# Two buffers for the column marks, one PSUM tile for both halves of the count, and the count one slot later

## The chip, the cores and the metric

One core of a Trainium2 chip runs the whole network as one launch. The metric is the time on the device in microseconds (us), for the slowest core, which here is the only one.

## What is computed

Four graph layers run over the same 4096 nodes of 256 features and the same 4096 x 4096 matrix `adj`; each ends in a layer norm. The change lies in layer 1, in the first of its two attention steps:

```python
def _top_p_attention(X, W1, W2, W3):
    q = X @ W1.T @ W2.T
    k = X @ W3.T
    probs = jax.nn.softmax(q @ k.T / TAU, axis=-1)
    idx = jnp.argsort(-probs, axis=-1)
    sp = jnp.take_along_axis(probs, idx, axis=-1)
    cs = jnp.cumsum(sp, axis=-1)
    keep_sorted = cs - sp < TOP_P            # 0.9
    ...
    A = probs * mask
    return A / jnp.maximum(A.sum(-1, keepdims=True), 1e-12)
...
for n in range(2):
    A = _top_p_attention(Xa, W1, W2, W3)
    Xf = R @ Xf                              # R: adj-like matrix, rows sum to 1
    Xa = A @ Xa
    Z = Z + Xf @ U1[n].T + Xa @ U2[n].T
```

Each row keeps its largest probabilities until they sum to 0.9. In the first step few columns are kept, so the kernel lists the columns that any row of a block needs and gathers only those.

## The kernel before

**Blocks and steps.** The first attention step is a stage of its own. It handles 32 blocks (`I`) of 128 rows. `narrow(I)` is a Python generator that writes one block's instructions; each `yield` ends a step. A loop by hand advances every live block by one step in each slot, the oldest block first, and starts a new block every 8 slots (`SLOTS`). A block lives about 42 slots, so five or six blocks are interleaved, and eight slots make a round. Beside them `r_stream()` advances 1.15 steps a slot (`PACE`): it gathers rows of `qtab` by lists (`xg`, on POOL, line 379) and multiplies them into `acc` (line 1156) three of its own steps later (`LATE`). For the later blocks it also gathers `pc`, blocks of `adj`. The order on PE, ACT, DVE and POOL is the order written (`manual_schedule`); only the DMAs on SP are placed by the scheduler.

**A block's steps around the change**, numbered from its start:

- 0 to 8: logits `lg` of 2 x 512 columns on PE (line 1014), their exp `e` on ACT (1029), and the eight largest of each 256 columns on DVE (`cand`, 1020), four times.
- 9 and 10: the 40 largest are sorted on DVE (`top`, `rest`), and a threshold `mid` between the last kept and the first dropped is found. `ex` is the running sum of the 40; POOL copies its last value to `f_x` (1043).
- 11 to 15: the change is here. ACT writes `marks` = sign(mid - e) in bf16 for 2048 of the 4096 columns (1056). PE counts them: for each 128 columns, `marks` is the weight and a column of ones the moving operand, so that column `b` of `cs` has the sum over the 128 rows (1060). A sum of 128 means that no row keeps that column, so `has = cs < 127.5` on DVE (1062) says which columns are listed. Both halves of 2048 go through one `marks` buffer, one after the other: marks in step 11, count in 12, `has` and the second marks in 13, second count in 14, second `has` in 15, followed by a running sum `upto` (1064) and `rank`.
- 16 to 20: small matmuls `pd` (1070 to 1072), ACT copies `off` and `step`, DVE `since` (1081), small matmuls `pi` (1085), and on DVE five operations that end in `idx` (1094), the list of columns.
- 21 to 23: five gathers `g<-tab,idx` on POOL (379), 128 rows each.
- 25 to 41: `pk` transposes (1106), `kg`, `sl` (1112), `w`, `pw` (1126), `wT`, `psa` (1133, tile `acc`), `xa`, `ptx` (236), `xT` (239), `po` (464), `v`, `z`, `psq` (285).

**Who meets whom in a slot.** By the order written, in slots 0 to 7 of a round PE has: `psq`, `pd`, `lg`; then `psa`, `pk`; `lg`; `ptx`, `sl`, `pi`; the first count `cs`, `lg`; `po`; the second count, `lg`; `pw`. The matmuls of `r_stream` lie between these. The first count of block I (step 12) stands in the slot in which block I-1 is at step 20, the DVE work that ends in `idx`.

**PSUM and SBUF.** `tp_tile` takes the bank of tag `tp`, of which this stage has one: `cs`, `pd` and `pi` follow each other in it, so each waits until DVE or ACT has read the one before. `lg`, `pk`, `sl` and `pw` share two tiles of tag `lg`. The pool `sp` has two buffers for each tile unless `bufs` says otherwise. `iota` makes constant tiles in a given pool, two of them in pools of two buffers; `reload` loads a row block by SP, in `r_stream` as `xin<-qp` (851), three buffers.

Of the kernel before, what the change touches and what calls it, by code (L numbers as in the profile page):

```python
# [11 lines left out]
F32 = mybir.dt.float32  # L12
BF16 = mybir.dt.bfloat16
I32 = mybir.dt.int32
AF = mybir.ActivationFunctionType
OP = mybir.AluOpType
AX = mybir.AxisListType

P = 128
N = 4096  # L20
D = 256
# [48 lines left out]
def gnn_kernel(ctx: ExitStack, tc: tile.TileContext, x, pair, W0, W1, W2T, W3T, U1T, U2T,  # L70
               ln_g, ln_b, Hv, W3L, b3, out):
    nc = tc.nc
# [3 lines left out]
    work = ctx.enter_context(tc.tile_pool(name="work", bufs=2))  # L76
# [3 lines left out]
    scopes, pools = [], {}  # L80
# [21 lines left out]
    def bank(shape, name, tag):  # L102
        return pools["psum"].tile(shape, F32, name=name, tag=tag, bufs=n_banks.get(tag, 1))
# [10 lines left out]
    def one(name, dtype=F32, bufs=2):  # L114
        return small.tile([P, 1], dtype, name=name, tag=name, bufs=bufs)

    def rows(I):
        return slice(I * P, (I + 1) * P)
# [4 lines left out]
    for j in range(NT):  # L123
        t = big.tile([P, D + 1], F32, name=f"xw_{j}", tag=f"xa{j}", padded_shape=[P, D + 2])
# [26 lines left out]
    edge = const.tile([P, NT], F32, name="edge")  # L151

    def iota(shape, name, pattern, base=0, mult=0, pool=const):
        t = pool.tile([P] + shape, F32, name=name)
        nc.gpsimd.iota(t, pattern, base=base, channel_multiplier=mult, allow_small_or_imprecise_dtypes=True)
        return t

    iota8 = iota([8], "iota8", [[1, 8]])
    down8 = const.tile([P, 8], F32, name="down8")
    nc.vector.tensor_scalar_mul(down8, iota8, -1.0)  # L160
    iota16 = iota([LE], "iota16", [[1, LE]])
    place = iota([512], "place", [[1, 512]], base=1, pool=pools["tmp"])
    row = const.tile([P, 1], I32, name="row")
    nc.gpsimd.iota(row, [[1, 1]], base=0, channel_multiplier=1)
# [682 lines left out]
        return nb  # L847

    def reload(src, I, name="xin", pool=None):
        t = (pools[pool] if pool else work).tile([P, D], F32, name=name, bufs=2 if pool else 3)  # L850
        nc.sync.dma_start(t, src[rows(I), :D])
        return t

# [91 lines left out]
    def r_ahead(a, to):  # L945

        I = a["I"]
        psr = acc_tile("R")
        blocks = [pc[:, k, :] for pc, (a0, b0) in zip(unpack(I), pieces(I)) for k in range(b0 - a0)]
        rest = [reload(ttab, I, "told", "w2"), reload(zd[I], 0, "zold", "w2")]  # L950
        xs = []

        def fetch():
            if len(xs) < CAPS[I]:
                xs.append(pools["gat"].tile([P, D], F32, name="xg", padded_shape=[P, D + 2]))
                gather(xs[-1], ttab, idx_x, col(I, len(xs) - 1))

        for _ in range(AHEAD):
            fetch()
        yield  # L960
        for n in range(CAPS[I]):
            nc.tensor.matmul(psr[:, :D], blocks[n], xs[n][:, :D], start=(n == 0), stop=False)
            fetch()
            if n < CAPS[I] - 1:
                yield
        for n, t in enumerate(rest):
            nc.tensor.matmul(psr[:, :D], ident, t, start=False, stop=(n == 1))
        to["xf"] = scaled_rest(a, psr)
# [14 lines left out]
    ones_bf = const.tile([P, 1], BF16, name="ones_bf")  # L983
    nc.vector.memset(ones_bf, 1.0)
    ranks = []
    for k in range(2):
        t = const.tile([P, N // P + 1], BF16, name=f"ranks_{k}")
# [3 lines left out]
    def tp_tile(shape, name):  # L991
        return bank(shape, name, "tp")
# [3 lines left out]
    def narrow(I):  # L996


        sp, at_I = pools["sp"], slice(I, I + 1)
# [5 lines left out]
        e = pools["e"].tile([P, N], F32, name="e")  # L1005
        sq = small.tile([P, NC], F32, name="s4", bufs=3)
        nb, per = N // P, LC // SEG0
# [41 lines left out]
        mid = one("mid0", bufs=5)  # L1049
        nc.vector.tensor_scalar(mid, u, v, 0.5, op0=OP.add, op1=OP.mult)  # L1050
        yield
        has = sp.tile([P, nb], F32, name="has")
        m = nb // 2
        for half in (slice(0, m), slice(m, nb)):
            marks = sp.tile([P, m * P], BF16, name="marks", bufs=1)
            nc.scalar.activation(marks, e[:, half.start * P:half.stop * P], AF.Sign, bias=mid, scale=-1.0)
            yield
            cs = tp_tile([P, m], "cs")
            for b in range(m):
                nc.tensor.matmul(cs[:, b:b + 1], marks[:, b * P:(b + 1) * P], ones_bf, start=True, stop=True)  # L1060
            yield
            nc.vector.tensor_scalar(has[:, half], cs, P - 0.5, None, op0=OP.is_lt)
        upto = sp.tile([P, nb], BF16, name="upto")
        nc.vector.tensor_tensor_scan(upto, ones.to_broadcast([P, nb]), has, 0.0, op0=OP.mult, op1=OP.add)
        rank = ranks[I % 2]
# [45 lines left out]
        for a, b in ((0, LC), (LC, NB * P)):  # L1111
            nc.tensor.matmul(sl[:, a:b], qi[:DA, :], kg[:, a:b], start=True, stop=True)
        x0 = reload(tab, I, "x0r", "w1")
        yield
        w = sp.tile([P, NB * P], F32, name="w", bufs=1)
# [29 lines left out]
    def r_one(b, after):  # L1145

        first = b < LE
        old = reload(qpd[b], 0)
        es = es_tile()[:, 0, :] if first else None
        packs = None if first else unpack(b)  # L1150
# [49 lines left out]
    with tc.manual_schedule(engines=everything):  # L1200
        active, side, credit, n = [], r_stream(), 0.0, 0
        started = 0
        while active or started < NT:
            if n % SLOTS == 0 and started < NT:
                active.append(narrow(started))
                started += 1
            for g in list(active):
                if next(g, active) is active:
                    active.remove(g)
            credit += PACE  # L1210
            while credit >= 1.0:
                next(side, None)
                credit -= 1.0
            if n % 2:
                next(lists, None)
            n += 1
        run(side)
# [118 lines left out]
    for I in range(NT):  # L1336
        t = big.tile([P, D + 2], F32, name=f"x2_{I}", tag=f"xa{I}")
# [190 lines left out]
```

## Time and profile before

| | |
|---|---|
| median of 3 runs | 2875.66 us (2869.0 to 2879.26) |
| profiled execution | 2874.88 us; its span in the trace 2873.0 us |
| stage of the first attention step | first exp at 536 us, last count at 1256 us |
| stretch 733 to 1236 us of it, 23 rounds | PE 419.12, DVE 359.71, ACT 290.08, POOL 349.88 us busy of 503; granted clock 0.86 |
| 1300 us to the end | PE 1248.28, DVE 1240.73, ACT 1065.99, POOL 1138.05 us busy of 1573; granted clock 0.92 |

A round is counted here from the first count of one block to that of the next. A line of the profile names the line of code, the engine, the operation and its tiles (out<-in). Behind the bar stand the busy time and the mean of one, then the idle time of that engine just before, and what ended it. PEld is the weight load, which may run ahead of the matmuls. The granted clock is the share of TensorE's full rate that the chip allowed.

### The profile page before, as it was taken

How to read it: one execution, taken by the hardware profiler on the slowest of the kernel's cores; microseconds unless marked ns; L12 is line 12 of the kernel's file. 1: busy time of each engine (PE TensorE's matmuls, PEld its weight loads, DVE VectorE, ACT ScalarE, POOL GpSimd, SP SyncE). 2: the span in 40 equal slices, each digit the busy share in tenths (PEclk: the TensorE clock that was granted, in tenths of full speed). 3: DMA queues.
4: the chain of work that ended last, by engine and by line, in shares of the span. 5: the costliest groups of instructions: out<-in, count | busy, mean ns of one | idle time of the engine just before them, and what ended most of it. 6: DMA issues, size and time to landing. Idle time of an engine off the chain costs nothing.

```text
span 2873.0 us, 38144 instructions
## 1 busy us (share of the span) xinstructions
PE 2277.4 (79%) x10712; PEld 1607.6 (56%) x10712; DVE 2111.7 (74%) x6474; ACT 1520.8 (53%) x2432; POOL 1775.8 (62%) x2840
## 2 busy tenths in 40 slices
PE   6768798677888888883678888888888887587897
PEld 4556676344544444440456666666666566476685
DVE  4777566777776767641778899999999997377574
ACT  0001111344555556546778888888989983354111
POOL 1003545265676766732678888888888784575774
PEclk9999899878888888885799999999999998799998
DMA  9995665344444544430111111111111111686664
GB/s 262 285 267 167 195 197 159 120 140 136 132 137 134 144 132 139 136 92 29 52 61 55 57 51 50 56 51 45 47 43 59 39 36 55 207 240 207 186 209 125
DMA packets 354060, 354.25 MB, mean 123 GB/s; under 512 B 35120, under 2 KB 307008, under 8 KB 353840
## 3 DMA queue, kind: packets, MB, share of 16 engines
q1 hardware_dynamic: 272224, 183.10, 21.8%
q0 software_dynamic: 51008, 144.85, 17.6%
q10 hardware_dynamic: 30608, 23.77, 2.6%
q8 instruction: 88, 1.44, 0.2%
q14 instruction: 132, 1.08, 0.1%
HBM read 298.69 MB, written 52.89 MB: 122 GB/s over the span
## 4 chain that ended last, share of the span: by engine, by line
PE 18%; DVE 13%; ACT 10%; POOL 8%; issue 5%; DMA 3%; SPq 0%; DVEq 0%; ACTq 0%; POOLq 0%
PE psa L228 4%; DVE cand L759 3%; ACT junk L676 3%; PE acc L433 3%; PE acc L1359 2%; PE lg L569 2%; DVE tmp L753 2%; PE pz L866 2%; ACT junk L678 2%; ACT e L637 2%; ACT junk L640 2%; POOL xg L379 1%; PE acc L204 1%; DVE top L736 1%; DVE rest L738 1%
## 5 line engine op out<-in xcount | busy, mean ns | idle before, releaser
L228 PE MATMUL psa<-v,eT 128*128 128x256 f32 x2048 | 513.3, 398 | 90.1 <-ACT eT L219 90.1
L228 PEld LDWEIGHTS psa<-v,eT 128*128 128x128 f32 x2048 | 400.4, 199 | 171.1 <-ACT eT L219 116.1
L204 PE MATMUL acc<-xw,panel 128*128 128x257 f32 x1024 | 258.1, 408 | 67.4 <-DMA panel<-in_pair 61.1
L379 POOL DMA_INDIRECT xg<-in_x,idx_x x72 | 69.6, 966 | 325.3 <-DVE idx_a L356 240.8
L204 PEld LDWEIGHTS acc<-xw,panel 128*128 128x128 f32 x1024 | 202.7, 203 | 119.4 <-issue 42.8
L676 ACT ACTIVATE junk<-e,h 128x4096 bf16<-128x4096 f32 x64 | 237.4, 3709 | 34.8 <-POOL h L656 29.2
L678 ACT ACTIVATE junk<-e,h 128x4096 bf16<-128x4096 f32 x64 | 238.3, 3723 | 0.1
L217 PE MATMUL pt<-ident,e 128*128 128x128 f32 x1024 | 158.3, 285 | 80.7 <-DVE e L805 53.6
L379 POOL DMA_INDIRECT xg<-ttab,idx_x x180 | 177.1, 984 | 71.2 <-issue 35.4
L1020 DVE MAX8 cand<-e 128x8 f32<-128x256 f32 x512 | 179.3, 412 | 55.7 <-ACT e L1029 50.4
L379 POOL DMA_INDIRECT g<-tab,idx x160 | 156.8, 980 | 101.3 <-PE cs L1060 49.0
L569 PE MATMUL lg<-kT,qi 64*128 64x512 f32 x512 | 157.4, 693 | 69.6 <-ACT junk L640 67.0
L379 POOL DMA_INDIRECT pc<-in_pair,idx_a x180 | 172.9, 961 | 63.3 <-issue 48.4
L379 POOL DMA_INDIRECT xg<-qtab,idx_x x180 | 175.5, 975 | 55.6 <-issue 42.3
L759 DVE MAX8 cand<-tmp 128x8 f32<-128x128 f32 x1024 | 203.2, 275 | 1.2
L217 PEld LDWEIGHTS pt<-ident,e 128*128 128x128 f32 x1024 | 130.6, 147 | 125.5 <-issue 84.4
L219 ACT COPY eT<-pt 128x512 f32<-128x512 f32 x256 | 144.7, 591 | 85.4 <-PE pt L217 85.1
L239 ACT COPY xT<-ptx 128x256 f32<-128x256 f32 (+1 forms) x96 | 42.3, 440 | 268.0 <-PE ptx L236 142.0
L379 POOL DMA_INDIRECT xg<-x3d,idx_x x146 | 138.9, 951 | 65.9 <-issue 38.1
L1014 PE MATMUL lg<-kT,qi 64*128 64x512 f32 x512 | 171.1, 749 | 6.8 <-DMA qi<-q 5.1
L1156 PE MATMUL acc<-xg,pc 128*128 128x256 f32 x360 | 135.5, 473 | 47.2 <-DMA xg<-qtab,idx_x 35.4
L637 ACT ACTIVATE e<-lg 128x1024 f32<-128x1024 f32 x128 | 131.5, 1027 | 71.6 <-PE lg L569 67.8
(323 smaller groups left out, 5670.3 us busy)
## 6 DMA issues: line engine op xcount, KB each, us to landing
panel<-in_pair SPq DMA_DIRECT2D x200, 256.0 KB
half<-in_pair SPq DMA_DIRECT2D x64, 512.0 KB
pc<-pk SPq DMA_DIRECT2D x55, 320.0 KB
pc<-pk SPq DMA_DIRECT2D x45, 256.0 KB
tab<-xi ACTq DMA_DIRECT2D x33, 160.0 KB
pc<-pk SPq DMA_DIRECT2D x23, 192.0 KB
x2d<-x SPq DMA_DIRECT2D x32, 129.0 KB
x<-x2d SPq DMA_DIRECT2D x32, 129.0 KB
```

The costliest lines, as they stand in the source:

```text
L204: nc.tensor.matmul(ps[:, :width], a[:, k, :], r, start=(j == 0), stop=stop and j == NT - 1)
L217: nc.tensor.transpose(pt[:, k, :], e[:, (g * 4 + k) * P:][:, :P], ident)
L219: nc.scalar.copy(eT[g], pt)
L228: nc.tensor.matmul(ps[:, :D], eT[g][:, k, :], rhs[j][:, :D], start=(j == 0), stop=stop and j == NT - 1)
L379: nc.gpsimd.indirect_dma_start(out=o, out_offset=None, in_=src, in_offset=bass.IndirectOffsetOnAxis(ap=idx[:, c], axis=0))
L569: nc.tensor.matmul(ps[:, h, :], qi[r, :], kT[r, (n * NC + c) * LC:][:, :LC], start=True, stop=True)
L637: nc.scalar.activation(both(e, c), ps, AF.Exp, accum_out=s8[:, c:c + 1])
L676: nc.scalar.activation(junk_tile(), e, AF.Relu, bias=h, scale=-1.0, accum_out=part)
L678: nc.scalar.activation(junk_tile(), e, AF.Sign, bias=h, scale=-1.0, accum_out=below)
L759: nc.vector.max(cand[:, c * (NS // 2) + g, :], w[:, g * SEG:(g + 1) * SEG])
L1014: nc.tensor.matmul(lgs[c][:, k, :], qi[r, :], kT[r, c * LC:(c + 1) * LC], start=True, stop=True)
L1020: nc.vector.max(cand[:, b, :], e[:, b * SEG0:(b + 1) * SEG0])
```

## The change

- Both marks are made in consecutive steps, 11 and 12, each into its own buffer of `sp` (two by default, 4 KB per partition more).
- `cs` is one tile of 32 columns for both halves. The two counts stand in steps 13 and 14. There was a count in 12 and in 14 before, so the first moves by one step and the second stays.
- `has` is one operation on 32 columns in step 15, in place of two on 16 columns.
- The number of steps stays 42. To make room, `iota` asks for one buffer, and `reload` for two everywhere (three before for `xin<-qp`).

```diff
     def iota(shape, name, pattern, base=0, mult=0, pool=const):
-        t = pool.tile([P] + shape, F32, name=name)
+        t = pool.tile([P] + shape, F32, name=name, bufs=1)
...
     def reload(src, I, name="xin", pool=None):
-        t = (pools[pool] if pool else work).tile([P, D], F32, name=name, bufs=2 if pool else 3)
+        t = (pools[pool] if pool else work).tile([P, D], F32, name=name, bufs=2)
...
         has = sp.tile([P, nb], F32, name="has")
         m = nb // 2
-        for half in (slice(0, m), slice(m, nb)):
-            marks = sp.tile([P, m * P], BF16, name="marks", bufs=1)
-            nc.scalar.activation(marks, e[:, half.start * P:half.stop * P], AF.Sign, bias=mid, scale=-1.0)
+        parts = (slice(0, m), slice(m, nb))
+        marks = []
+        for half in parts:
+            marks.append(sp.tile([P, m * P], BF16, name="marks"))
+            nc.scalar.activation(marks[-1], e[:, half.start * P:half.stop * P], AF.Sign, bias=mid, scale=-1.0)
             yield
-            cs = tp_tile([P, m], "cs")
+        cs = tp_tile([P, nb], "cs")
+        for half, mk in zip(parts, marks):
             for b in range(m):
-                nc.tensor.matmul(cs[:, b:b + 1], marks[:, b * P:(b + 1) * P], ones_bf, start=True, stop=True)
+                c = half.start + b
+                nc.tensor.matmul(cs[:, c:c + 1], mk[:, b * P:(b + 1) * P], ones_bf, start=True, stop=True)
             yield
-            nc.vector.tensor_scalar(has[:, half], cs, P - 0.5, None, op0=OP.is_lt)
+        nc.vector.tensor_scalar(has, cs, P - 0.5, None, op0=OP.is_lt)
         upto = sp.tile([P, nb], BF16, name="upto")
```

On the engines, PE has `pi`, `lg`, `po`, count, count, `lg` where it had `pi`, count, `lg`, `po`, count, `lg`, sometimes with matmuls of `r_stream` between. ACT keeps `w`, second marks, `e`, except that `y` of `r_stream` (857) changes sides with a marks in a few rounds. POOL keeps its order. On SP the loads `xin<-qp` go one block later, and a few neighbours change places.

## Prediction

> **What bounds the kernel now.** The change touches only the first attention step, so I read that stage: first the page for the clock and the costliest gathers, then the answer for the tile `cs`, then the waits of a steady stretch, then single rounds in order of time.
>
> ```profile
> PEclk9999899878888888885799999999999998799998
> ...
> L379 POOL DMA_INDIRECT g<-tab,idx x160 | 156.8, 980 | 101.3 <-PE cs L1060 49.0
> ```
>
> The clock row stands at 7 and 8 over the stage (slices 8 to 18 of 40, 72 us each): TensorE has its full rate only part of the time. The gathers of `g` seem to wait for `cs`. They don't read it; they read `idx`, which ends in the same moment, as the rounds below show, so I count this as a wait for `idx`, which the change doesn't touch.
>
> ```profile
> L1060 PE MATMUL cs<-ones_bf,marks x1024: 162/164/212, 557.3 to 1256.2; 128*128 128x1 bf16 x171
> ...
> its engine sat idle before it (us, times) until:
>   DVE idx L1094: 52.9, 24
>   ACT w L1116: 11.0, 6
>   ACT marks L1056: 5.6, 4
> ...
> who waited for it (us, times):
>   POOL g L379: 49.0, 29
>   ACT marks L1056: 20.9, 17
> ```
>
> PE stands 69.5 us before the counts, nearly all before the first half. That is the single `tp` bank: `cs` may not be written before DVE has read the older block's `pi`, and its last reader is `idx`. In each of rounds 1 to 30 `idx` ends 0.14 or 0.15 us before the first count starts, whatever the profile names. The second marks wait 20.9 us for the first count: that is the single `marks` buffer. Then the steady stretch: its busy times of PE, PEld, DVE, ACT and POOL, the granted clock and the DMA share, and its waits (us in total, times, longest).
>
> ```profile
> 733.00:1236.00 503.00, 419.12 (x2336) 240.87 (x2338) 359.71 (x1283) 290.08 (x520) 349.88 (x419) 0.86 0.48 138
> ```
>
> ```profile
> PE cs L1060 <- DVE idx L1094: 33.9, 18, 3.8
> PE acc L1156 <- DMA xg<-qtab,idx_x: 31.5, 25, 6.0
> ...
> POOL f_x L1043 <- DVE ex L1042: 20.4, 13, 3.4
> ```
>
> In these 23 rounds (21.8 us each) PE is busy 419 of 503 us, so it idles 84: 46 before counts (33.9 and what is put down to ACT), 31.5 for gathered rows. **Two loops go through a round.** One is PE's own order. The other is: `idx`, then POOL's gathers of `g` and `xg` in their order, the landing, the `acc` matmul, the rest of PE's order up to `pi`, `idx`. POOL needs some 14.2 gathers a round of about 0.97 us and 0.30 us between two, 18 us, and 1.5 us of small work. Pairing each `xg` gather with its matmul, I find one that starts within 0.7 us of the landing (about 3.15 us after the gather's start) in 20 of the 23 rounds. So the second loop is the one that mostly binds, and the wait at `cs` lies outside it: it comes after `idx`, and before the point at which PE meets the gathered rows.
>
> ```profile
> 1002.58 1.22 PE L1156 MATMUL acc<-xg,pc 128*128 128x256 f32 x2 [4.61 <-DMA xg<-qtab,idx_x]
> ...
> 1054.41 1.13 PE L1014 MATMUL lg<-kT,qi 64*128 64x512 f32 x4
> ...
> 1060.18 0.57 PE L1060 MATMUL cs<-ones_bf,marks 128*128 128x1 bf16 x16 [1.77 <-DVE idx L1094]
> 1060.68 2.08 PE L1014 MATMUL lg<-kT,qi 64*128 64x512 f32 x4
> ```
>
> The same four matmuls take 1.13 us, or 2.08 after an idle PE: at 1059.4 to 1066.2 the granted clock is 0.50, from 1066.3 to 1079.7 it is 1.00. A clock of 0.86 in the stretch means half rate for 28% of it. Now most spells begin at the count and slow `lg` and `po`; where PE waited 3.4 to 6.0 us for rows instead (the rounds from 859, 991, 1016 and 1145), the spell fell on what follows.
>
> **What the Trainium skill says.** "Perfetto Trace Analysis", Optimization Strategy, takes a gap that repeats as a sign of too few SBUF or PSUM buffers; the gap at `cs` is that, in every round. "PSUM — Partial Sum Buffer", Engine vs sequencer instructions: matmuls start and complete in program order. The trace agrees: `lg`, which needs nothing of `cs`, starts 0.5 us after it. "TensorE: Matmul & The Clock Gate", What's actually happening: half rate after an idle window of about 3.4 us. This trace differs in part: spells of 3.4 or 6.8 us begin after waits of only 1.6 to 2 us too, when small matmuls stand around them. The measurement decides.
>
> **The change part by part.**
> - *First count a slot later.* Removes the wait for `idx`: `po` now covers it. `lg` goes first, and needs ACT's `e` of the step before. Per round the gain behind the counts is the old start of `lg`, less the later of PE's idling start and the end of that `e`, less 0.5 us for the 16 count matmuls now behind `po`. Over rounds 1 to 30: 20 rounds gain, 0.5 to 3.3 us, 32.3 together; ten, where `e` ends as late as the count started, lose 0.1 to 0.4, 2.5 together. Net 29.8 us, if nothing else bound.
> - *What of it arrives.* Rounds 3, 6, 15, 23, 24 and 30 show no wait for rows behind the counts: 1.15, 1.16, 0.99, 1.78, 1.78 and 1.91, less 0.24 in round 25: 8.5 us. In rounds with a row wait PE only comes early to it. Some comes back through POOL: an earlier second `lg` brings `ex` and so `f_x` earlier, of which POOL waits 20.4 us in 13 of the steady rounds. The smaller of gain and this wait, over all rounds not counted yet, is 9.6 us; I take half, 5, since a later row must also need it. Together -13.5 us.
> - *The idle moves.* In ten steady rounds (those from 754, 774.5, 817, 839, 885.5, 927.5, 951, 1040, 1060 and 1170) a gain of 0.9 us or more meets a wait for rows of `xg` or `g` of 0.2 to 2 us. Where `lg` and `po` ran at half rate, PE gets through them up to 2.5 us sooner as well. Round 1040: `lg` at -1.9 us, `po` to 1.3, counts to 2.6, and with `lg`, `pw`, `psq`, `pd`, `lg` and one `acc`, PE stands at 8.1 before rows that land at 10.7. That wait of 2.6 us (1.0 before) is followed by half rate on `psa`, `pk` and `sl`, inside the second loop. A spell of 3.4 us of full work costs 1.7 us, one of 6.8 costs 3.4; mean 2.55, ten times: +25.5 us. Bounds: 0, or 3.4 us in all 23 rounds, 78 us.
> - *Two marks buffers.* The second marks lose their wait, 20.9 us; behind them `e` and `pw` come sooner, which the row waits then take: 0, at most -5.
> - *One `has`.* 32 operations of 158 ns fewer, the other some 10 ns longer (from `since`: 547 ns for 640 columns). 5 us of an engine 72% busy, and the last count still stands before it: 0, at most -2.
> - *`xin` with two buffers.* The load waits for the `y` two blocks back, not three; on SP it stands beside the store of that same `y`, so nothing queues longer, and two blocks of four gathers (10 us) remain for it: 0, at most +5. `iota`: only memory.
>
> Sum: -13.5 + 25.5 = **+12 us**. Against the profiled execution, 2874.88, that is 2886.9; it lies 0.8 us under the median, so against the median 2887.7. I take **2887 us**.
>
> **The rivals.**
> - *The wait becomes time saved.* PE is the bound, POOL follows `idx` as PE brings it forward, and a PE without the gap keeps its clock. The whole 29.8 us arrive: 2846 us. For it: PE is the busiest engine, and POOL itself idles for `idx`. Against: 31.5 us of waits for rows. It decides from the point at which at most five of the ten rounds get a new spell: 13.5 us of gain are more than five times 2.55.
> - *Nothing moves.* The row waits take the gain, and spells only change places: 2870 to 2880 us. For it: rounds 7 to 29 whose `lg` behind the count ran at full rate took 22.1 us on average (8), those at half rate 21.6 (15): a PE faster there did not shorten rounds. Against: the four rounds with row waits of 3.4 us and more took 25.2 us, the other nineteen 21.1.
> - *It doesn't do what it says.* If the wait for `idx` still stands before the first count behind `po`, only the order changes: 2876 us. Against: `po` ends 3.9 us or more after the old count's start in all steady rounds.
>
> **How the numbers follow.** About 0.3%, 8.6 us, is what a measurement of this kernel tells from no change. The moved idle: 0.50, of which 0.42 is slower and 0.08 within. Nothing moves, or no effect: 0.26, of which 0.02 lies on each side. Time saved: 0.24, of which 0.20 is faster. So faster 0.22, same 0.34, slower 0.44. Range: 2852 (most of the time saved) to 2910 (spells that cost 3.4 us in the ten rounds and no gain, 34 us).
>
> **What would show it.** Right: the first count has no wait for `idx`; PE's waits for `xg` grow from 31.5 us to 50 or more in the steady rounds; `psa` groups of ten take over 4 us (2.3 at full rate) more often; the stage ends about 10 us later. The later stages keep their lengths. Wrong: row waits as before with a clock above 0.86 and rounds near 20.5 us (time saved); or `lg` waiting for `e` in most rounds, which would put the 0.5 us of the moved count on the path.

## The result, and the profile after

The changed kernel takes 2875.93 us (median of 20 runs, 2867.03 to 2882.73), the kernel before 2874.9 us beside it (20 runs, 2865.84 to 2882.02). The ratio is 1.0005 with a 95% interval of 0.9994 to 1.0015: no difference that can be measured. The forecast was 2887 us. The profiled execution of the changed kernel took 2872.45 us, 2.4 us less than that of before. From its first exp to its last `idx` the stage took 731.4 us before and 732.0 after; ahead of it and behind it these two executions differ by -8.5 and +5.5 us.

The page of the changed kernel shows nearly the same clock in the stage (slices 8 to 18). The gathers of `g` no longer seem to wait for `cs`, but POOL stands longer before them in all, 119.5 us after 101.3:

```profile
span 2870.6 us, 38110 instructions
...
PEclk9999898777888888885799999999999998799899
...
L379 POOL DMA_INDIRECT g<-tab,idx x160 | 155.6, 972 | 119.5 <-issue 79.4
```

The answer for the tile `cs` shows that the change does what it says. PE stood 69.5 us before the counts; now no engine but DVE stands before any line of this tile, and that for 1.9 us. `has` is one operation in place of two.

```profile
L1064 PE MATMUL cs<-ones_bf,marks x1024: 163/163/211, 550.5 to 1247.8; 128*128 128x1 bf16 x171
L1066 DVE TENSOR_SCALAR has<-cs x32: 172/181/194, 557.0 to 1248.0; 128x32 f32<-128x32 f32 x32
its engine sat idle before it (us, times) until:
  PE cs L1064: 1.9, 4
```

Now the steady stretch in the answer by windows (span, then busy time of PE, PEld, DVE, ACT and POOL, granted clock, DMA share) and its waits (us in total, times, longest):

```profile
733.00:1236.00 503.00, 414.98 (x2332) 237.56 (x2331) 359.05 (x1260) 289.73 (x523) 348.57 (x417) 0.88 0.49 137
```

```profile
PE acc L1160 <- DMA xg<-qtab,idx_x: 45.0, 27, 6.4
PE pk L1110 <- DMA g<-tab,idx: 21.6, 14, 3.1
PE lg L1014 <- ACT e L1029: 15.6, 13, 2.9
```

Two of these waits before, in the same view of the same stretch:

```profile
PE pk L1106 <- DMA g<-tab,idx: 2.8, 2, 1.5
PE lg L1014 <- ACT e L1029: 1.5, 3, 0.5
```

The clock granted in this stretch is 0.88 in place of 0.86. PE idles 503 - 415 = 88 us here, after 84 before. The 46 us before the counts have gone, and three other waits stand in their place: for rows of `xg` 45.0 (31.5 before), for rows of `g` at `pk` 21.6 (2.8 before), for `e` at `lg` 15.6 (1.5 before).

**One round, before and after.** These are PE's groups of the same block in order of time (start, duration, engine, line, operation, tiles; in brackets the idle time before it and what ended it). Before, its `idx` ends at 1060.0 us and the next at 1081.2:

```profile
1060.18 0.57 PE L1060 MATMUL cs<-ones_bf,marks 128*128 128x1 bf16 x16 [1.77 <-DVE idx L1094]
...
1071.35 2.43 PE L1133 MATMUL acc<-g,wT 128*128 128x256 f32 x10
1073.61 0.71 PE L1106 MATMUL pk<-ident,g 128*64 128x128 f32 x5
...
1076.66 1.34 PE L1112 MATMUL sl<-kg,qi 64*128 64x512 f32 x4
1077.94 0.29 PE L1085 MATMUL pi<-step,since 128*128 128x34 bf16 x5
```

In the changed kernel the same `idx` ends at 1056.1 us and the next at 1077.7:

```profile
1058.68 0.54 PE L1064 MATMUL cs<-ones_bf,marks 128*128 128x1 bf16 x16
...
1063.86 2.43 PE L1137 MATMUL acc<-g,wT 128*128 128x256 f32 x10
1066.12 0.60 PE L1110 MATMUL pk<-ident,g 128*64 128x128 f32 x4
1068.93 0.30 PE L1110 MATMUL pk<-ident,g 128*64 128x128 f32 x1 [2.20 <-DMA g<-tab,idx]
1069.16 1.13 PE L1014 MATMUL lg<-kT,qi 64*128 64x512 f32 x4
1071.86 1.22 PE L1160 MATMUL acc<-xg,pc 128*128 128x256 f32 x2 [1.57 <-DMA xg<-qtab,idx_x]
...
1073.43 2.50 PE L1116 MATMUL sl<-kg,qi 64*128 64x512 f32 x4
1075.87 0.32 PE L1089 MATMUL pi<-step,since 128*128 128x34 bf16 x5
```

`psa` (line 1137, tile `acc<-g,wT`) starts 7.8 us after `idx` in place of 11.3: PE gained 3.5 us. Four of the five transposes `pk` run at once; the fifth waits 2.20 us for the last gathered rows of `g`. Then come a wait for `xg` and half rate on `sl` (2.50 us in place of 1.34). `pi` is at its end 20.1 us after `idx`, 18.2 before. The gain has become a loss of 1.9 us; the five DVE operations behind `pi` follow at once here and not before, which takes 1.5 us off, and the round is 21.6 us long after 21.2.

**All 23 steady rounds.** Round n goes here from the nth `idx` to the next. Adding PE's records by place, rounds 7 to 29, gives this (us; the waits are gaps between matmuls):

| stretch of a round | before | after | difference |
|---|---|---|---|
| `idx` to the start of `psa` | 283.3 | 255.7 | -27.6 |
| `psa` to the end of `pi` | 164.1 | 203.5 | +39.4 |
| end of `pi` to `idx` | 54.2 | 44.6 | -9.6 |
| sum | 501.6 | 503.8 | +2.2 |

The +39.4 are 21.5 of waits (`pk` for `g` from 3.0 to 21.6, `xg` from 3.4 to 6.1) and 17.9 of the same number of matmuls taking longer: `sl` 29.4 to 35.1, `acc<-xg,pc` 16.9 to 21.3, `lg` 26.1 to 29.5, `pk` 13.5 to 15.8, `psa` 58.0 to 59.2. The -9.6 is DVE: the five operations themselves take 32.7 us before and 32.9 after, but from the end of `pi` to the first of them it is 21.5 before and 11.7 after, with 8.1 us of `cand`, `er`, `es` and `pr` behind the end of `pi` in place of 17.5.

**Where the loop closes.** The last of the five gathers of `g` starts 9.73 us after `idx` before and 9.67 after: the change doesn't move it. Where `pk` waits, its rows land about 4 us after that start. So `pk` can't end before some 13.8 us. In the kernel before, the last `pk` started a median of 1.1 us after that landing (the landing taken as 3.95 us after the gather's start). That is all that could be gained ahead of `pk` in most rounds. After, the median is 0.5 us: in 12 of the 23 rounds the last `pk` starts within 0.6 us of the landing, in 5 before. In nine of the other eleven PE had stood 1.1 to 6.4 us for rows of `xg` ahead of `psa`. So the changed kernel runs into gathered rows in nearly every round, those of `g` in some and those of `xg` in others.

### The profile page after: what moved, and what is told of

It reads as the page before. It is cut to its first block, busy times and chain, and to the rows that moved or that the text cites. A ratio compares the mean times of both kernels' runs of the same rounds, so it can differ in the third digit from the quotient of the medians.

```text
span 2870.6 us, 38110 instructions
## 1 busy us (share of the span) xinstructions
PE 2279.5 (79%) x10712; PEld 1604.9 (56%) x10712; DVE 2111.6 (74%) x6442; ACT 1520.6 (53%) x2432; POOL 1781.8 (62%) x2840
## 4 chain that ended last, share of the span: by engine, by line
PE 18%; DVE 17%; ACT 8%; POOL 6%; issue 4%; DMA 3%; DVEq 0%; SPq 0%; POOLq 0%; ACTq 0%
PE psa L228 4%; DVE cand L759 4%; PE acc L1363 3%; PE acc L433 3%; DVE tmp L753 3%; ACT junk L676 2%; PE lg L569 2%; PE pz L866 2%; DVE e L805 2%; DVE e L801 2%; DVE top L736 2%; DVE rest L738 1%; ACT junk L678 1%; PE acc L204 1%; ACT e L637 1%
## 5 line engine op out<-in xcount | busy, mean ns | idle before, releaser
L676 ACT ACTIVATE junk<-e,h 128x4096 bf16<-128x4096 f32 x64 | 237.4, 3709 | 30.7 <-POOL h L656 26.1
L379 POOL DMA_INDIRECT g<-tab,idx x160 | 155.6, 972 | 119.5 <-issue 79.4
L1160 PE MATMUL acc<-xg,pc 128*128 128x256 f32 x360 | 146.7, 503 | 72.0 <-DMA xg<-qtab,idx_x 53.7
```

Source lines behind the costliest of these rows:

```text
L379: nc.gpsimd.indirect_dma_start(out=o, out_offset=None, in_=src, in_offset=bass.IndirectOffsetOnAxis(ap=idx[:, c], axis=0))
L676: nc.scalar.activation(junk_tile(), e, AF.Relu, bias=h, scale=-1.0, accum_out=part)
L1160: nc.tensor.matmul(acc[0][:, :D], block, x[:, :D], start=(k == 0), stop=(k == CAPS[b] - 1))
```

## The experiments

Ratios are to the kernel before on the same chip, in brackets the 95% interval. "A round" is the mean of rounds 7 to 29 of the profiled execution: 21.81 us before, 21.90 after.

### Does PE's order bind? Each half counted twice

```diff
-            for b in range(m):
+            for b in 2 * list(range(m)):
```

> The kernel after with each half counted twice: 32 more matmuls of one column per block, about 1.05 us more on PE each round, behind po. Loop of gathers (idx, POOL, landing, acc or pk, pi, idx): PE only comes later to rows it waits for, 87 us of idle in the steady rounds, so 0 to +8 us. PE's own order as the bound: 31 rounds of 1.05 us, +33 us. Clock spells as the cause of the lost gain: a shorter wait means fewer spells, -5 to -20 us.

Measured: 2866.6 us against 2869.91, 0.9985 [0.9973, 0.9998]; a round 21.98 us. So the 33 us of PE's own order are out, but the time lies a little under the range of the loop of gathers too. Sixteen more matmuls take 0.40 us (0.94 us for 32 after 0.54), so the doubled counts put some 18.4 us more of PE work between `idx` and `psa`, and that stretch grew by 14.5 us. Behind `psa` 13.9 us came back: 5.4 us of shorter waits, nearly all for `g`, and 8.5 us because the matmuls ran faster. The waits of PE in the steady stretch:

```profile
PE acc L1160 <- DMA xg<-qtab,idx_x: 34.2, 24, 5.8
...
PE pk L1110 <- DMA g<-tab,idx: 16.4, 9, 3.1
```

So 0.8 us a round of PE's time ahead of `psa` can be given away at no cost. The time that the change saves, 1.2 us a round, is of the same kind, and worth as little. This run alone doesn't show that all of it is slack: the busier PE ran less at half rate (174 us in the stage in place of 218.5), which paid for part of the extra work.

### Does the loop of the gathers bind? The addition `xb` on POOL three times

```diff
-        nc.gpsimd.tensor_add(xb, x0, bb)
+        for _ in range(3):
+            nc.gpsimd.tensor_add(xb, x0, bb)
```

> The kernel after with the add that makes xb on POOL written three times: 2 x 0.74 us more on POOL in each round, between the gathers of g. Loop of gathers: nearly all of it arrives, 31 x 1.47 us, +30 to +46 us. PE's own order as the bound: POOL has room of some 3 us a round, 0 to +8 us. DVE and ACT (the chain from lg over the sort and mid to e) as the bound: 0 to +8 us.

Measured: 2919.62 us, 1.0158 [1.0132, 1.0185]; a round 23.71 us. `xb` stands among the gathers of `g`: the last of these now starts 11.23 us after `idx` in place of 9.67, 1.56 later, and the round is 1.81 us longer. In the stretch from 733 to 1236 us the wait at `pk` grew from 21.6 to 35.9 us:

```profile
PE acc L1161 <- DMA xg<-qtab,idx_x: 45.1, 18, 6.1
PE pk L1111 <- DMA g<-tab,idx: 35.9, 21, 3.0
```

The delay of 1.5 us on POOL reaches the round in full, where 0.8 us on PE did not. Nor is it POOL's total that is full: before the first gather of `g` POOL stood 54.8 us in these 23 rounds, after 49.4 without the two additions. Together the two runs show that the round hangs on the gathers and not on PE's order ahead of `psa`. This run delays `xg` too, so it doesn't tell the two kinds of rows apart.

### Take away the wait for `xg`: its rows multiplied five steps later, on both kernels

```diff
-    LATE, PACE = 3, 1.15
+    LATE, PACE = 5, 1.15
```

On the kernel before:

> The kernel before with LATE 5 in place of 3: the acc matmuls stand two steps of the row stream later behind their gathers. Loop of gathers: PE's waits for xg, 31.5 us in the steady rounds, shrink to under 10, and 10 to 30 us are saved, less what the wait for rows of g at pk takes over. PE's own order, or DVE and ACT, as the bound: 0 to -8 us, since the waits only move.

On the changed kernel:

> The kernel after with LATE 5 in place of 3. Loop of gathers: the waits for xg, 45.0 us in the steady rounds, shrink to under 10; since PE no longer stands before the counts either, the saving is larger than that of LATE 5 alone on the kernel before, by up to the 30 us that the change itself was to bring: 20 to 50 us under the kernel before. If the e of ACT behind the marks is the bound instead: not over 8 us apart from LATE 5 on the kernel before.

Measured: on the kernel before 2833.85 us, 0.9871 [0.9849, 0.9892], a round 20.33 us; on the changed kernel **2822.77 us, 0.9830 [0.9806, 0.9855]**, a round 20.12 us. The second is 47 us under the kernel before; the changed kernel itself was not run on this chip. PE's waits from 733 to 1236 us, on the kernel before:

```profile
PE cs L1060 <- DVE idx L1094: 46.9, 22, 3.8
PE pk L1106 <- DMA g<-tab,idx: 12.0, 13, 1.9
...
PE acc L1156 <- DMA xg<-qtab,idx_x: 0.8, 1, 0.8
```

and on the changed kernel:

```profile
PE pk L1110 <- DMA g<-tab,idx: 44.8, 32, 4.0
PE lg L1014 <- ACT e L1029: 25.1, 14, 2.7
...
PE acc L1160 <- DMA xg<-qtab,idx_x: 0.5, 1, 0.5
```

The waits for `xg` are gone in both, and still the change brings only 11.1 us (2833.85 less 2822.77; the five runs of each don't overlap), not the 29.8 us that it takes from PE's order by the prediction's count. In the profiled pair the stage is 17.1 us shorter (679.5 after 696.6), of which 8.0 lie in rounds 1 to 6 and only 4.8 in the 23 steady ones. There the sum by place is the same picture again: `idx` to `psa` -38.1 us, `psa` to `pi` +38.6 (of which `pk` for `g` +25.3), `pi` to `idx` -5.4. In all 23 rounds of the last kernel the last `pk` starts within 0.6 us of the landing of `g`, and in 18 rounds of the kernel before with `LATE` 5. With `xg` out of the way, what the change meets at `pk` is plain: a place that was at its limit in most rounds already. POOL's total is near as well: 14.1 gathers of 1.27 us and 1.5 us of small work, 19.4 us, in a round of 20.12. In 9 of the 23 rounds it goes on to the first `g` with no more than its usual 0.30 us between two gathers.

### The buffers without the move: first count back in step 12

The remaining runs were on four other chips, on which the kernel before takes 3134.54 to 3150.65 us where several engines stop together now and then (shown at the end of this section); only ratios within a chip are used.

```diff
             nc.scalar.activation(marks[-1], e[:, half.start * P:half.stop * P], AF.Sign, bias=mid, scale=-1.0)
-            yield
+            if half.start == 0:
+                yield
...
                 nc.tensor.matmul(cs[:, c:c + 1], mk[:, b * P:(b + 1) * P], ones_bf, start=True, stop=True)
             yield
+            if half.start == 0:
+                yield
```

> The change without its move: both marks made early in two buffers, one cs tile and one has, xin with two buffers, but the first count back in step 12, before lg and po. Loop of gathers: the wait for idx before the count is back, about 46 us in the steady rounds, and the time is that of before, -6 to +6 us. If the buffers or the one has were worth something by themselves, -10 us or more; if the loads of xin with two buffers cost, +5 us or more.

Measured: 3149.21 us against 3147.86, 0.9995 [0.9978, 1.0013]. The wait for `idx` is back before the count, though with 15.9 us and not the 46 expected:

```profile
PE cs L1065 <- DVE idx L1101: 15.9, 12, 1.8
```

Two marks buffers, one `cs`, one `has` and two buffers for `xin` are worth nothing that can be measured, there at least.

### Give `pk` a slot more, with `LATE` 5

```diff
+        yield
         kg = sp.tile([DA, NB * P], F32, name="kg", bufs=1)
...
         nc.vector.reciprocal(rk, k)
-        yield
         yield
```

On the kernel before, then on the changed one:

> The kernel before with LATE 5, and the steps pk, kg, sl, w one slot later (the empty step behind rk is taken out for it). Beside LATE 5 alone, which saved 36 us: its waits for g at pk are 10.9 us, so 0 to 10 us more are saved; PE still stands before the counts in every round.

> The kernel after with the same two moves. Loop of gathers: LATE 5 alone left 38.0 us of waits for g at pk in 24 rounds. With pk a slot later they go too, and the change comes to its own 20 to 30 us against the same two moves on the kernel before. If the e behind the marks (27.4 us of waits of lg) is the next bound: at most 12 us, as between the two with LATE 5 alone (11 us).

Measured: 0.9967 [0.9945, 0.9990] and 0.9984 [0.9966, 1.0003]; again on another chip 0.9979 [0.9959, 0.9999] and 0.9977 [0.9950, 1.0004]. The two don't differ. On these chips a steady round takes 24 to 27 us in the profiled executions, so PE has time to spare at `pk` whatever the order, and what a later `pk` is worth stays open.

### POOL's small operations on DVE

All four of them (`xb`, `tgt`, `f_x`, `n_listed`):

```diff
-        nc.gpsimd.tensor_add(xb, x0, bb)
+        nc.vector.tensor_add(xb, x0, bb)
...
-        nc.gpsimd.tensor_scalar(tgt, s, TOP_P, None, op0=OP.mult)
+        nc.vector.tensor_scalar(tgt, s, TOP_P, None, op0=OP.mult)
...
-        nc.gpsimd.tensor_copy(x, ex[:, K0 - 1:])
+        nc.vector.tensor_copy(x, ex[:, K0 - 1:])
...
-        nc.gpsimd.tensor_tensor(n_listed[:, at_I], off, mine, OP.add)
+        nc.vector.tensor_tensor(n_listed[:, at_I], off, mine, op=OP.add)
```

> The kernel after with xb, tgt, f_x and n_listed made on DVE in place of POOL, LATE 3. POOL loses 1.4 us of work a round and the stalls behind f_x. Loop of gathers: 1.0 to 1.4 us a round, 30 to 45 us saved, the mirror of xb made three times (+46 us against the kernel after). PE's order or DVE as the bound: 0, or up to +15 us, for DVE gets about 0.9 us more a round.

Measured: 3337.98 us, 1.0584 [1.0554, 1.0614]. The expectation missed by far: a round takes 32.4 us. In its waits from 800 to 1500 us DVE stands for ACT before `n_listed`, and 152 us before `has` for something that the profile doesn't name:

```profile
DVE has L1066 <- remote: 152.2, 15, 15.8
...
DVE n_listed L1082 <- ACT off L1079: 45.9, 19, 8.2
```

Only `tgt` and `f_x` on DVE, with `LATE` 5 and `pk` a slot later, and then without the latter:

> The same with tgt and f_x made on DVE in place of POOL. With LATE 5 alone DVE waited 16.5 us for tgt behind the gathers and POOL 6.3 us for ex. Loop of gathers, and the sort chain to mid and e as the next bound: both gain, 8 to 20 us under the kernel without this edit. PE's order as the bound: -3 to +3 us.

> The changed kernel with gathered rows multiplied five steps later, and tgt and f_x of the first attention step on DVE in place of POOL. POOL then has two small operations less a block and no longer waits for ex (11.9 us in 23 rounds of the changed kernel). If POOL's order sets the round once rows come early: ratio 0.975 or less to the kernel before (0.983 without the edit). If the way from idx over g to the transposes sets it: 0.980 to 0.985, as without. If DVE's queue becomes the wait: 0.99 or more.

Measured: 0.9948 [0.9926, 0.9969], best on its chip, and 0.9923 [0.9892, 0.9955], best on its own. Beside 0.9977 without the two on DVE, on the chip of the former, this hints that taking two operations that wait for DVE out of POOL's queue helps there; the two intervals overlap. Whether it adds to the 0.9830 above is open.

### Fewer half-rate spells: the last logits written twice

```diff
-            for k, r in enumerate(halves):
-                nc.tensor.matmul(lgs[c][:, k, :], qi[r, :], kT[r, c * LC:(c + 1) * LC], start=True, stop=True)
+            for _ in range(2 if c == NC - 1 else 1):
+                for k, r in enumerate(halves):
+                    nc.tensor.matmul(lgs[c][:, k, :], qi[r, :], kT[r, c * LC:(c + 1) * LC], start=True, stop=True)
```

> The kernel after with the last lg of each block (step 6, behind the counts) multiplied twice: 1.13 us more of full matmul work a round, where PE is about to wait for gathered rows. Half-rate spells as a cost of the round: PE stays busy, spells get fewer, -5 to -25 us. Loop of gathers alone: the work fits into PE's waits, -4 to +8 us. PE's own order as the bound: 31 x 1.13 us, +35 us.

> The changed kernel with the last logits matmuls of each block written twice (same result, 1.13 us more full-rate PE work a round, 36 us over the stage), so that fewer windows of PE are idle enough to bring half rate. If the moved half-rate spells cost what the prediction said (up to 25.5 us), and the extra work keeps half of them away: 10 us faster than the changed kernel, some 2863 us where the kernel before takes 2875. If the gather loop sets the round and spells lie under its waits: equal within 0.3%, though half rate falls by 10 us or more. If PE's own order is tight: up to 36 us slower, 2911 us.

With `LATE` 5:

> The changed kernel with gathered rows multiplied five steps later in place of three, and the last logits matmuls written twice. With early rows PE's order is closer to the bound. If spells cost nothing there either and PE still has slack at the transposes of g: as the same kernel without the doubling, ratio 0.983 to the kernel before, within 0.3%. If the clock is what is left: faster, ratio 0.975 to 0.98. If PE's order is now the bound: slower by up to 36 us, ratio up to 0.995.

Measured: 1.0065 [1.0046, 1.0083], 1.0028 [1.0009, 1.0047], and 1.0009 [0.9989, 1.0028]. None is faster. But with rounds of 25 us, PE is idle so often that half rate came to 154 to 166 us of the rounds past their first 8 us, more than the 83 us of the changed kernel on the first chip: the extra work kept no spells away. The price of a spell is not settled by these.

### The gathers of `g` all in one step, with `LATE` 5

```diff
             gather(g[k], tab, idx, slice(k, k + 1))
-            if k % 2:
-                yield
+        yield
+        yield
         yield
         yield
```

> The kernel before with gathered rows multiplied five steps later, and the five gathers of g issued in one step in place of 2, 2 and 1. The last gather then starts about 5.3 us after idx in place of 9.9, and lands at about 9.2. In the kernel before, the wait for idx at the count still holds PE back, and psa and pk come at 11 us and later: the waits of pk for g (12.0 us in 23 rounds) go, and the round gets at most 0.5 us shorter. If the place of the gathers binds: ratio 0.98 to 0.987 to the kernel before. If POOL's total binds: no change beside the same kernel with its gathers spread (0.987). If the rows of qtab then come late: 0.99 or more, and waits for xg are back.

> The changed kernel with gathered rows multiplied five steps later, and the five gathers of g issued in one step. If the landing of g is what the change ran into: the waits of pk for g (44.8 us in 23 rounds with the gathers spread) go to under 10 us, and this kernel is 20 to 30 us faster than the same edits on the kernel before (11 us with the gathers spread), ratio 0.970 to 0.975. If POOL's total sets the round (14.2 gathers of 1.27 us and 1.5 us of small work, 19.5 us): rounds stay at 20.1 us and the ratio at 0.983. If rows of qtab or e of ACT take the gain: waits for xg or e of 30 us or more, ratio 0.98.

Beside them, the gathers spread:

> The changed kernel with gathered rows multiplied five steps later and its gathers spread, again, on the chip of the two kernels with the gathers together, so that these stand beside it: 0.983 as before if this chip is like the first; nearer 0.995 if it is one that runs everything slower. All theories expect the same.

Measured: 1.0077 [1.0048, 1.0106] on the kernel before, 1.0121 [1.0077, 1.0165] on the changed one, 1.0014 [0.9993, 1.0035] with the gathers spread. The last gather starts 6.0 us after `idx`, and `pk` waits for nothing, as expected. No kernel became faster, because `pk` there came 6 us (median) after the landing of `g` even with the gathers spread. One of the stops in the run with the gathers spread, on ACT and on DVE:

```profile
1026.72 1.02 ACT L1029 ACTIVATE e<-lg 128x1024 f32<-128x1024 f32 x1 [8.29 <-remote]
```

```profile
1026.66 0.19 DVE L1066 TENSOR_SCALAR has<-cs 128x32 f32<-128x32 f32 x1 [7.78 <-remote]
```

Both engines resume in the same moment, 7 us after PE had finished the counts that `has` reads (1019.3 us). Where such stops set the round, the loop of the gathers doesn't, so these runs don't test it.

## Why the prediction was wrong

The forecast of +12 us was a sum of two terms of opposite sign. The rival "Nothing moves" (2870 to 2880 us) gave the right time, and its mechanism, row waits that take the gain, is nearer to the traces too: in the steady stretch PE's waits grew by 13.5 us at `xg` and by 18.8 at `pk`. Each term can be held against the rounds that it named, in this one pair of profiles.

- **First count a slot later: right.** The wait for `idx` is gone, and `po` and `lg` cover it. PE reaches `psa` 27.6 us sooner in the 23 steady rounds.
- **What of it arrives, -13.5 us: in part.** The seven rounds that stood for -8.5 us (3, 6, 15, 23, 24, 25 and 30) became 7.6 us shorter together. That the sum fits is partly luck: round 3 grew by 0.9, round 6 fell by 2.7, and in rounds 15, 24, 25 and 30 PE met new waits of 0.9 to 1.9 us at `pk`. The 5 us through `f_x` don't show: the nine steady rounds in neither list changed by 0.2 us together. I took the 2.8 us of waits of `pk` for `g` as slack. It was nearly a bound: `pk` had a median of 1.1 us before it would wait.
- **The idle moves, +25.5 us: the failed step.** The ten rounds named grew by **6.5 us together, 0.65 each where the forecast had 2.55**. The waits and the half rate did come: in these ten rounds PE stood 12.1 us longer for `xg` and 10.7 longer for `g` at `pk`, and in the steady rounds half rate later than 8 us after `idx` went from 39.6 to 83.0 us (in the first 8 us from 103.8 to 39.9, so that there is less of it in all). But `pi` ended only 14.4 us later in the ten rounds, and 7.9 of these came back between `pi` and `idx`. The prices were added one by one, as if every wait and every spell reached `idx` and DVE stood ready behind `pi`. It didn't: with `pi` later, DVE had done more of its other work.
- Over all 23 steady rounds `idx` to the end of `pk` became 5.4 us shorter (360.1 to 354.7), the end of `pk` to that of `pi` 17.2 longer, and `pi` to `idx` 9.6 shorter. The sum is +2.2 us, and the medians differ by 1.0 us, within what can't be told from nothing.
- **`has`, marks buffers, `xin`: 0 each, right** as far as the run without the move shows it (0.9995).
- **"Time saved" fell,** and not for want of waits at `xg` alone: without them the change is worth 11.1 us.
- **What would show it:** no wait for `idx` at the count, yes; waits for `xg` of 50 us, no, 45.0, since `pk` took the rest; `psa` over 4 us, no: its groups took 2.68 us on average after 2.63, with two of 23 over 4 us in both; the stage 10 us longer, no, 0.6.

Shown are the place of the bound (doubled counts against tripled `xb`) and that the change ends in a wait for `g` once `xg` is early. Only read from two traces are the 9.6 us of DVE and the share of the half rate; what a half-rate spell costs by itself is not shown. Open is what the change brings when the gathers of `g` are early too. My estimate from POOL's 19.4 us of a round of 20.12, 0.7 us in each of 31 rounds, is that not much over 20 us more can come before POOL itself is full.

## What to carry to other kernels

A wait that repeats in every round is worth nothing by its length; its worth is the slack of the next thing that the freed engine meets, so measure for each later wait how long its data had been there before (here 1.1 us), the short waits above all. "Perfetto Trace Analysis", Optimization Strategy, in the Trainium skill says that such a gap can mean too few buffers. Here one PSUM bank did stand behind it, but moving the count, and not a buffer, took it away, and its removal alone gave a ratio of 1.0005. Before building, double the work that stands in the gap and add a microsecond to the suspected loop: here 0.8 us a round on PE cost nothing, and 1.5 us on POOL cost 1.8.

## What the runs showed of the hardware

- Rows gathered by an indirect DMA on POOL (0.97 us an instruction, 0.30 us between two) were there 3.5 to 4.9 us after the start of the last gather of `g` where `pk` waited for them, in the six traces of the first chips; for `xg` I had read 3.15 us.
- The amount of half rate did not set the round: over 536 to 1260 us it was 229.8 us before, 218.5 after and 174 with doubled counts, with rounds of 21.81, 21.90 and 21.98 us. The last of these kernels has more PE work in exchange, so this doesn't say that half rate is free.
- The same program took 2870 to 2876 us where the first runs were made, and 3135 to 3151 on four other chips. Instructions had the same durations there (medians of `marks` 2.00 us, `cand` 0.41 us and gathers 0.95 us in both); in this stage the time went into stops of several engines at once, of up to 12.0 us in the run with `LATE` 5 and the gathers spread. What ends them the traces don't name.
